# B and C products over 2048 columns, and one tile for the copies of dt·x, in a selective-scan layer

## The chip, the cores and the metric

The kernel runs on one core of a Trainium2 chip. A core has five engines with instruction streams of their own: PE (TensorE, matrix products), DVE (VectorE, elementwise work and scans), ACT (ScalarE, functions such as exp), POOL (GpSimd) and SP (SyncE, which here issues nearly all DMAs). They meet through semaphores. Each engine takes its instructions in a fixed order. The metric is the device time of one execution, in microseconds.

## What is computed

A decoder layer over 8 sequences of 512 tokens with 512 features, in three stages with a residual and a layer norm after each: a selective state-space layer (Mamba), a cross attention with 16 heads, and a mixture of 32 experts. The change lies in the first stage, whose core is this (D_INNER 1024 channels, 16 states a channel):

```python
dt = softplus(dt @ dt_proj_w + dt_proj_b)
dA = exp(A[None, None] * dt[..., None])
dBx = dt[..., None] * B_ssm[:, :, None, :] * x_main[..., None]

def scan_fn(h, inp):
    dA_t, dBx_t, C_t = inp
    h = dA_t * h + dBx_t
    y_t = einsum('bdn,bn->bd', h, C_t)
    return (h, y_t)

y = y + x_main * D_param
y = y * silu(z)
out = res_scale * (y @ out_proj_w) + residual
```

So each of 1024 x 16 states runs through a first-order recurrence over time. Its input is the product of dt·x with B, and its output is multiplied with C and summed over the states.

## The kernel before

**Chunks and steps.** The eight sequences are cut into 16 chunks of T = 256 tokens. A chunk takes 32 steps (q, g, jj): q = 0 to 3 picks 256 channels, g = 0 to 3 picks 4 of the 16 states, jj = 0 or 1 picks half of the channels. A step's tiles have 128 partitions, 32 channels x 4 states, and NB = 4 blocks of 256 tokens, each with one more column ahead of it that carries the old state in. There are 512 steps in all. Two steps that differ in jj alone are called a group here (256 of them), and passing on to the next q a change of q (63 of them).

**A step** consists of these parts:

- `carry` (L484) takes an h tile of 4 x 257 columns (six buffers) and copies the old state into the first column of each block, on ACT.
- `decays` (L475) writes exp(A·dt) into one of two tiles `das`, four ACT instructions over 256 columns (L480).
- `steps_in` (L491) is the B product: dt·x times B into h, on DVE, 1024 columns (L494).
- `scan` (L498) runs the recurrence on DVE over 4 x 257 columns (L501).
- `keep` (L503) saves the last column for the next chunk, on ACT.
- `collect` (L508) is the C product: h times C in place, on DVE, 1024 columns (L510). After the one with jj = 1 it hands back `products` (L516): four matmuls that sum the states of both h tiles with the matrix `fold` into `py` (L521). They are called a step later.

**Copies.** Since a channel lies on four partitions, dt and dt·x are spread by DMA. `prepare` (L432) computes dt and dt·x for 256 channels (its DVE part is L457 to L460) once for each q. `repeat` (L422) then copies them into tiles `rep`, 128 x 1024 columns of 4 bytes, each by two DMAs of 256 KB on SP (L428). For each q there are four such tiles: dt and dt·x, each for jj = 0 and 1. All of them share five buffers. `bcast` (L412) spreads the rows of B and C in a like manner, once a chunk.

**Order.** The main loop (from L1099) writes down in each step: the B product, a third of the side work, the scan, then carry and decays of the next step, another third, the products of the group before, the C product, and the last third. Side work is everything else: projections and convolution of the next chunk, gate and output projection of the chunk before, and the attention of the sequence before (`units`, L753), which has maxima over scores on DVE (L815), exponentials on ACT (L843) and small DMAs on SP (L799 to L803, L829, L875). `repeat` is called at k%8 = 5 and 6, where k counts the steps of a chunk; the next q's first step is k%8 = 0.

This written order is not the order of execution. The tile framework reorders the instructions of each engine when it builds the program: it takes the ready instruction that stands first, by its own estimate of times, and adds all semaphores. So DVE often runs two B products, two scans and two C products in a row.

Of the kernel before, what the change touches and what calls it, by code (L numbers as in the profile page):

```python
# [8 lines left out]
F32 = mybir.dt.float32  # L9
# [3 lines left out]
ALU = mybir.AluOpType  # L13
# [4 lines left out]
P = 128  # L18
# [9 lines left out]
T = 256  # L28
NT_ = T // P
NG = NST // 4  # L30
NQ = 4
QP = P // NQ
NB = 4
# [55 lines left out]
def layers(ctx, tc, a, x1d, filld, based, xbuf):  # L89
# [23 lines left out]
    nc = tc.nc  # L113

    mp = ctx.enter_context(tc.tile_pool(name="l_mamba", bufs=1))
    bcp = ctx.enter_context(tc.tile_pool(name="l_bc", bufs=2 * NST // NG))
    cp = ctx.enter_context(tc.tile_pool(name="l_const", bufs=1))
# [73 lines left out]

    conv_tail = cp.tile([P, CC, 3], F32, name="l_conv_tail")
    state = cp.tile([P, CC // 2, NG, 2, NB], F32, name="l_state")
    nothing = cp.tile([P, NB, 1], F32, name="l_nothing")
    nc.gpsimd.memset(nothing, 0.0)
    das = [mp.tile([P, NB, T + 1], F32, name=f"l_da{i}") for i in range(2)]
    for da in das:
# [30 lines left out]
    first = cp.tile([P, E], F32, name="l_first")  # L228
    nc.gpsimd.iota(first, pattern=[[CAP, E]], base=-SLOTS, channel_multiplier=0, allow_small_or_imprecise_dtypes=True)
    first = first.unsqueeze(1).to_broadcast([P, SC, E])  # L230
# [181 lines left out]
    def bcast(f, g):  # L412

        got = []
        for r0 in (g, NST + g):
            t = bcp.tile([P, T], F32, tag="bc", name="bc")
            src = f["scr"].rearrange("(n s g) t -> n g s t", n=2, s=NQ)[r0 // NST, r0 % NST]
            nc.sync.dma_start(t, src.unsqueeze(0).to_broadcast([QP, NQ, T]))
            got.append(t.unsqueeze(1).to_broadcast([P, NB, T]))
        f["bc", g] = got  # L420

    def repeat(f, q, what, jj):  # L422

        f["rep", what, q, jj] = to = mp.tile([P, 2, 2, T], F32, tag="rep", name="rep", bufs=5)
        for j in range(2):
            r0 = (2 * jj + j) * QP
            src = f["ready", q][what][r0 : r0 + QP].rearrange("c i t -> c (i t)")
            nc.sync.dma_start(  # L428
                to[:, j].rearrange("p i t -> p (i t)"), src.unsqueeze(1).to_broadcast([QP, NQ, 2 * T])
            )  # L430

    def prepare(q, f):  # L432

# [40 lines left out]

    def decays(f, q, g, jj, da):  # L475

        dt = f["rep", 0, q, jj]
        for n in range(NB):
            j, i = n // 2, n % 2
            nc.scalar.activation(  # L480
                da[:, n, 1:], dt[:, j, i, :], AF.Exp, scale=aneg[:, 2 * q + i, 2 * jj + j, g : g + 1]
            )

    def carry(t, q, g, jj):  # L484

        last = state[:, q, g, jj].unsqueeze(2)
        h = mp.tile([P, NB, T + 1], F32, tag="h", name="h", bufs=6)
        nc.scalar.copy(h[:, :, 0:1], last if t else nothing)
        return h

    def steps_in(f, q, g, jj, h):  # L491

        dtx = f.pop(("rep", 1, q, jj)) if g == NG - 1 else f["rep", 1, q, jj]
        nc.vector.tensor_tensor(  # L494
            h[:, :, 1:], dtx.rearrange("p j i t -> p (j i) t"), f["bc", g][0], ALU.mult
        )

    def scan(da, h):  # L498

        flat = h.rearrange("p n t -> p (n t)")  # L500
        nc.vector.tensor_tensor_scan(flat, da.rearrange("p n t -> p (n t)"), flat, 0.0, ALU.mult, ALU.add)  # L501

    def keep(t, q, g, jj, h):  # L503

        if t < S // T - 1:
            nc.scalar.copy(state[:, q, g, jj].unsqueeze(2), h[:, :, T : T + 1])

    def collect(f, q, g, jj, h):  # L508

        nc.vector.tensor_tensor(h[:, :, 0:T], h[:, :, 1:], f["bc", g][1], ALU.mult)  # L510
        if jj == 0:
            f["half"] = h
            return
        hs, xs = (f.pop("half"), h), f["xs"][q]

        def products():  # L516
            if g == 0:
                f["py"] = psy.tile([P, 2, T], F32, tag="py", name="py")
                nc.tensor.matmul(f["py"], ident, xs, start=True, stop=False)
            for j in range(NQ):  # L520
                nc.tensor.matmul(  # L521
                    f["py"][j * QP : (j + 1) * QP, :, :],
                    fold,
                    hs[j // 2][:, 2 * (j % 2) : 2 * (j % 2) + 2, 0:T],
                    start=False,
                    stop=g == NG - 1,
                )

        return products
# [522 lines left out]
    steps = [(q, g, jj) for q in range(CC // 2) for g in range(NG) for jj in range(2)]  # L1052
# [19 lines left out]
    f = {"xt": x0}  # L1072
# [13 lines left out]
    n = 0  # L1086
    for g in range(NG):
        bcast(f, g)
    for what in range(2):
        for jj in range(2):  # L1090
            repeat(f, 0, what, jj)
    nc.scalar.activation(aneg, aneg, AF.Exp)
    nc.vector.tensor_scalar(aneg, aneg, -1.0, None, ALU.mult)
    decays(f, 0, 0, 0, das[0])
    ahead, products = carry(0, 0, 0, 0), None
    old, side, cleared, held = None, [], 0, None
    clock.append(0)

    for i, (b, t) in enumerate(chunks):  # L1099
        nf = {}  # L1100
        after = chunks[i + 1] if i + 1 < len(chunks) else None
# [5 lines left out]
        for k, (q, g, jj) in enumerate(steps):  # L1107
            if i and k == 1:
                bcast(f, NG - 1)
            if after and 28 <= k < 31:  # L1110
                bcast(nf, k - 28)
            qf, nq = (f, q + 1) if q + 1 < CC // 2 else (nf, 0)
            h = ahead

            parts = []

# [35 lines left out]
            def run(m):  # L1152
                clock[0] += 1
                settle()
                for x in thirds[m]:
                    if x[0] is do:
                        do(*x[1:-1], first=x[-1])
                    else:
                        x[0](*x[1:])

            steps_in(f, q, g, jj, h)
            more = qf is f or after
            if k % 8 == 6 and more:
                repeat(qf, nq, 0, 1)
            if k % 8 == 1:
                if k > 1:
                    gated(q - 1, f)
# [8 lines left out]
            if k == 5 and after:  # L1176
                load_x(*after, nf)
            run(0)
            scan(das[n % 2], h)
            n += 1  # L1180

            if k + 1 < len(steps) or after:
                then = steps[(k + 1) % len(steps)]
                ahead = carry(t if k + 1 < len(steps) else after[1], *then)
                decays(f if k + 1 < len(steps) else nf, *then, das[n % 2])
                if k % 8 == 5 and more:
                    repeat(qf, nq, 0, 0)
                    repeat(qf, nq, 1, 0)
                if k % 8 == 6 and more:
                    repeat(qf, nq, 1, 1)  # L1190
            if held:
                keep(*held)
            held = t, q, g, jj, h
            run(1)

            if products:
                products()
            products = collect(f, q, g, jj, h)
            run(2)
            while i < 2 and cleared < E * (i * len(steps) + k - 6) // (2 * len(steps) - 7):  # L1200
                clear(cleared)
# [5 lines left out]
        f = nf  # L1207
# [356 lines left out]
```

## Time and profile before

Three runs took 5404.84, 5407.18 and 5412.16 us, the median is 5407.18. The profiled execution took 5406.28 us; its span from the first to the last instruction is 5404.6 us, with a granted PE clock of 0.935.

| what | us | of the span |
|---|---|---|
| span of the profiled execution | 5404.6 | |
| PE busy | 4672.4 | 86% |
| DVE busy | 4235.9 | 78% |
| ACT busy | 2593.6 | 48% |
| PE weight loads | 2476.6 | 46% |
| POOL busy | 570.3 | 11% |
| DMA, queue of SP | | 41.1% of 16 engines |

The rows of 40 equal slices show where each engine is busy (in tenths; a slice is 135 us):

```profile
PE   6768889788888988988888888789999999999994
DVE  7999899989989989898998998943566555665554
ACT  5566565565656556566565655523222222222223
```

Up to slice 26 the scan section runs, with DVE at 8 or 9 tenths; behind it the experts run with PE at 9 tenths. A group's row in the page gives line, engine, operation, tiles (out<-in), partitions x columns and count, then busy time and the mean duration of one in ns, then the idle time of the engine just before and what ended it. In the timeline, a line with x2 joins two neighbours into one stretch; a bracket gives the idle time ahead of the instruction and who ended it. Matmul records can be missing here and there, so counts of PE are slightly low.

### The profile page before, as it was taken

Reading aid. Unit: us, or ns where it says so; the run is one execution under the profiler, and the core shown is the slowest. Engines: PE = TensorE matmul, PEld = TensorE weight load, DVE = VectorE, ACT = ScalarE, POOL = GpSimd, SP = SyncE. Lnnn points to the kernel's source line nnn. Section 1 sums busy time; section 2 is a strip of 40 time slices with the busy share of each in tenths; the row PEclk is TensorE's granted clock in tenths of the full one; section 3 lists DMA queues with packets and bytes.
Section 4 is the critical chain, followed back from the end, with each engine's and each line's share of the span. In section 5 each row is a group of like instructions: output and inputs, shape, how many; then the busy total and the mean of one; then the engine's idle time right before and its main releaser. Section 6 shows DMA issues by size and latency. Waiting matters only on the chain. (4 is left out here: it accounts for less than half of the span.)

```text
span 5404.6 us, 53991 instructions
## 1 busy us (share of the span) xinstructions
PE 4672.4 (86%) x17320; PEld 2476.6 (46%) x17320; DVE 4235.9 (78%) x5369; ACT 2593.6 (48%) x5726; POOL 570.3 (11%) x426
## 2 busy tenths in 40 slices
PE   6768889788888988988888888789999999999994
PEld 3324234234333423433333342333677777777773
DVE  7999899989989989898998998943566555665554
ACT  5566565565656556566565655523222222222223
POOL 1000002002000200200200020011111111111111
PEclk8879989999999999999999999899999999999997
DMA  8875346345444634634544463342344444544544
GB/s 236 266 224 146 87 96 208 81 114 176 114 104 117 197 77 109 189 98 107 174 125 100 117 200 78 91 146 66 103 128 127 123 117 118 127 127 121 129 115 144
DMA packets 486427, 719.03 MB, mean 133 GB/s; under 512 B 117137, under 2 KB 200625, under 8 KB 484096
## 3 DMA queue, kind: packets, MB, share of 16 engines
q1 hardware_dynamic: 450128, 627.16, 41.1%
q0 software_dynamic: 33280, 76.90, 7.5%
q10 hardware_dynamic: 2736, 11.54, 0.5%
q8 instruction: 137, 2.24, 0.2%
q14 instruction: 146, 1.20, 0.1%
HBM read 391.24 MB, written 165.05 MB: 103 GB/s over the span
## 5 line engine op out<-in xcount | busy, mean ns | idle before, releaser
L480 ACT ACTIVATE l_da<-rep,l_aneg 128x256 f32<-128x256 f32 x2048 | 895.0, 501 | 941.8 <-DVE h L501 877.0
L501 DVE TENSOR_TENSOR_SCAN h<-l_da,h 128x1028 f32<-128x1028 f32 x512 | 1166.0, 2292 | 20.3 <-ACT l_da L480 17.7
L494 DVE TENSOR_TENSOR h<-rep,bc 128x1024 f32<-128x1024 f32 x512 | 614.7, 1218 | 103.1 <-PE py L521 84.6
L510 DVE TENSOR_TENSOR h<-h,bc 128x1024 f32<-128x1024 f32 x512 | 619.5, 1217 | 2.1
L521 PE MATMUL py<-h,l_fold 128*32 128x512 f32 x2048 | 368.3, 644 | 113.4 <-DVE h L510 96.5
L813 PE MATMUL ps_s<-l_ka,l_qa 64*128 64x512 f32 x1024 | 325.6, 707 | 137.8 <-DVE mx L815 137.6
L1314 PE MATMUL ps_h<-xT,w 128*128 128x320 f32 x1536 | 435.8, 433 | 0.0
L1394 POOL DMA_INDIRECT based<-y,xe x160 | 255.5, 1597 | 1309.9 <-ACT y L1417 630.0
L1335 DVE TENSOR_TENSOR hT<-ps_h,p 128x320 f32<-128x320 f32 x128 | 62.9, 492 | 378.5 <-PE ps_h L1314 378.5
L815 DVE TENSOR_REDUCE mx<-ps_s 128x2 f32<-128x1024 f32 x256 | 310.2, 1217 | 58.5 <-PE ps_s L813 58.3
L1314 PEld LDWEIGHTS ps_h<-xT,w 128*128 128x128 f32 x1536 | 292.5, 191 | 118.3 <-issue 0.4
L855 PE MATMUL po<-eT,l_va 128*64 128x512 f32 x1024 | 301.5, 670 | 47.6 <-ACT eT L843 43.1
L839 PE MATMUL ps_t<-l_qa,l_ka 64*128 64x512 f32 x1024 | 308.4, 674 | 23.8 <-ACT eT L843 23.1
L843 ACT ACTIVATE eT<-ps_t 128x1024 f32<-128x1024 f32 x256 | 259.0, 1015 | 128.8 <-PE ps_t L839 128.5
L688 POOL DMA_INDIRECT xbuf<-x2t,dest x128 | 217.2, 1697 | 860.4 <-DVE dest L679 760.8
L1314 PE MATMUL ps_h<-t,s 128*128 128x320 f32 x1024 | 286.1, 432 | 0.0
L343 PE MATMUL ps_z<-xnT,wm 128*128 128x256 f32 x1024 | 238.0, 388 | 30.0 <-DVE o L561 24.3
L750 PE MATMUL ps_p<-x2T,wa 128*128 128x512 f32 x512 | 241.5, 626 | 18.1 <-ACT hT L944 10.4
L552 PE MATMUL po<-wm,zs 128*128 128x512 f32 x512 | 244.7, 632 | 13.8 <-DVE z L957 11.9
L343 PE MATMUL ps_x<-xnT,wm 128*128 128x256 f32 x1024 | 246.5, 393 | 4.5 <-ACT xnT L332 2.5
L343 PEld LDWEIGHTS ps_z<-xnT,wm 128*128 128x128 f32 x1024 | 194.6, 193 | 93.0 <-DVE o L561 37.5
L343 PEld LDWEIGHTS ps_x<-xnT,wm 128*128 128x128 f32 x1024 | 196.1, 195 | 80.5 <-issue 43.8
(232 smaller groups left out, 7170.4 us busy)
## 6 DMA issues: line engine op xcount, KB each, us to landing
w<-in_w SPq DMA_DIRECT2D x93, 1024.0 KB
wm<-in_in_proj_w SPq DMA_DIRECT2D x128, 512.0 KB
rep<-dt SPq DMA_DIRECT2D x256, 256.0 KB
rep<-dtx SPq DMA_DIRECT2D x256, 256.0 KB
xbuf<-zero SPq DMA_DIRECT2D x32, 1362.5 KB
xe<-xbuf SPq DMA_DIRECT2D x32, 1362.5 KB
wm<-in_out_proj_w SPq DMA_DIRECT2D x64, 512.0 KB
wa<-in_sw SPq DMA_DIRECT2D x24, 1024.0 KB
```

Source lines behind the costliest of these rows:

```text
L343: nc.tensor.matmul(ps[:, i, :], w[:, dc, i * P : (i + 1) * P], f["xnT"][:, dc, :], start=(dc == 0), stop=(dc == DC - 1),)
L480: nc.scalar.activation(da[:, n, 1:], dt[:, j, i, :], AF.Exp, scale=aneg[:, 2 * q + i, 2 * jj + j, g : g + 1])
L494: nc.vector.tensor_tensor(h[:, :, 1:], dtx.rearrange("p j i t -> p (j i) t"), f["bc", g][0], ALU.mult)
L501: nc.vector.tensor_tensor_scan(flat, da.rearrange("p n t -> p (n t)"), flat, 0.0, ALU.mult, ALU.add)
L510: nc.vector.tensor_tensor(h[:, :, 0:T], h[:, :, 1:], f["bc", g][1], ALU.mult)
L521: nc.tensor.matmul(f["py"][j * QP : (j + 1) * QP, :, :], fold, hs[j // 2][:, 2 * (j % 2) : 2 * (j % 2) + 2, 0:T], start=False, stop=g == N ...
L813: nc.tensor.matmul(ps[:, j, :], qa[r, lt * P : (lt + 1) * P], ka[r, :], start=True, stop=True)
L815: return lambda: nc.vector.tensor_reduce(mx[:, lt, :].unsqueeze(2), ps, AX.X, ALU.max) and None
L839: nc.tensor.matmul(ps[:, j, :], ka[r, kc * P : (kc + 1) * P], qa[r, :], start=True, stop=True)
L843: nc.scalar.activation(eT, ps, AF.Exp)
L855: nc.tensor.matmul(po[j * 2 * HD : (j + 1) * 2 * HD, :], va[:, kc, i, j * HD : (j + 2) * HD], eT[:, j, :], start=(kc == 0), stop=(kc == SC ...
L1314: nc.tensor.matmul(ps, w[:, n, r * P : (r + 1) * P], x[:, n, :], start=not more and n == 0, stop=n == 1, skip_group_check=more,)
```

## The change

The two steps of a group share one h tile of 2 x 4 blocks (2 x 4 x 257 columns, three buffers). The B product is done once a group, at jj = 0, over 8 x 256 = 2048 columns; the C product once a group, at jj = 1. `carry` and `keep` work on both halves at once, so they too are done once a group. Scans and decays remain single, each on its half of the tile.

The copies of dt keep tiles of 1024 columns (now three buffers). The copies of dt·x for both jj go into one tile `repx` of 2048 columns, with one buffer, by four DMAs that are now written down at k%8 = 6, right behind the B product of g = 3. The copies of dt stay at k%8 = 5 and 6. `products` of the group before are called at jj = 0.

```diff
 
     conv_tail = cp.tile([P, CC, 3], F32, name="l_conv_tail")
     state = cp.tile([P, CC // 2, NG, 2, NB], F32, name="l_state")
-    nothing = cp.tile([P, NB, 1], F32, name="l_nothing")
+    nothing = cp.tile([P, 2, NB, 1], F32, name="l_nothing")
     nc.gpsimd.memset(nothing, 0.0)
     das = [mp.tile([P, NB, T + 1], F32, name=f"l_da{i}") for i in range(2)]
     for da in das:
...
             t = bcp.tile([P, T], F32, tag="bc", name="bc")
             src = f["scr"].rearrange("(n s g) t -> n g s t", n=2, s=NQ)[r0 // NST, r0 % NST]
             nc.sync.dma_start(t, src.unsqueeze(0).to_broadcast([QP, NQ, T]))
-            got.append(t.unsqueeze(1).to_broadcast([P, NB, T]))
+            got.append(t.unsqueeze(1).to_broadcast([P, 2 * NB, T]))
         f["bc", g] = got
 
-    def repeat(f, q, what, jj):
-
-        f["rep", what, q, jj] = to = mp.tile([P, 2, 2, T], F32, tag="rep", name="rep", bufs=5)
-        for j in range(2):
-            r0 = (2 * jj + j) * QP
+    def copies(f, q, what, to, first):
+
+        for j in range(to.shape[1]):
+            r0 = (first + j) * QP
             src = f["ready", q][what][r0 : r0 + QP].rearrange("c i t -> c (i t)")
             nc.sync.dma_start(
                 to[:, j].rearrange("p i t -> p (i t)"), src.unsqueeze(1).to_broadcast([QP, NQ, 2 * T])
             )
+
+    def repeat_dt(f, q, jj):
+
+        f["dt", q, jj] = to = mp.tile([P, 2, 2, T], F32, tag="rep", name="rep", bufs=3)
+        copies(f, q, 0, to, 2 * jj)
+
+    def repeat_dtx(f, q):
+
+        f["dtx", q] = to = mp.tile([P, NQ, 2, T], F32, tag="repx", name="repx")
+        copies(f, q, 1, to, 0)
 
     def prepare(q, f):
 
...
 
     def decays(f, q, g, jj, da):
 
-        dt = f["rep", 0, q, jj]
+        dt = f["dt", q, jj]
         for n in range(NB):
             j, i = n // 2, n % 2
             nc.scalar.activation(
                 da[:, n, 1:], dt[:, j, i, :], AF.Exp, scale=aneg[:, 2 * q + i, 2 * jj + j, g : g + 1]
             )
 
-    def carry(t, q, g, jj):
-
-        last = state[:, q, g, jj].unsqueeze(2)
-        h = mp.tile([P, NB, T + 1], F32, tag="h", name="h", bufs=6)
-        nc.scalar.copy(h[:, :, 0:1], last if t else nothing)
+    def carry(t, q, g):
+
+        h = mp.tile([P, 2, NB, T + 1], F32, tag="h", name="h", bufs=3)
+        nc.scalar.copy(h[:, :, :, 0:1], state[:, q, g].unsqueeze(3) if t else nothing)
         return h
 
-    def steps_in(f, q, g, jj, h):
-
-        dtx = f.pop(("rep", 1, q, jj)) if g == NG - 1 else f["rep", 1, q, jj]
-        nc.vector.tensor_tensor(
-            h[:, :, 1:], dtx.rearrange("p j i t -> p (j i) t"), f["bc", g][0], ALU.mult
-        )
+    def steps_in(f, q, g, h):
+
+        dtx = f.pop(("dtx", q)) if g == NG - 1 else f["dtx", q]
+        wide = h.rearrange("p r n t -> p (r n) t")
+        nc.vector.tensor_tensor(wide[:, :, 1:], dtx.rearrange("p j i t -> p (j i) t"), f["bc", g][0], ALU.mult)
 
     def scan(da, h):
 
         flat = h.rearrange("p n t -> p (n t)")
         nc.vector.tensor_tensor_scan(flat, da.rearrange("p n t -> p (n t)"), flat, 0.0, ALU.mult, ALU.add)
 
-    def keep(t, q, g, jj, h):
+    def keep(t, q, g, h):
 
         if t < S // T - 1:
-            nc.scalar.copy(state[:, q, g, jj].unsqueeze(2), h[:, :, T : T + 1])
-
-    def collect(f, q, g, jj, h):
-
-        nc.vector.tensor_tensor(h[:, :, 0:T], h[:, :, 1:], f["bc", g][1], ALU.mult)
-        if jj == 0:
-            f["half"] = h
-            return
-        hs, xs = (f.pop("half"), h), f["xs"][q]
+            nc.scalar.copy(state[:, q, g].unsqueeze(3), h[:, :, :, T : T + 1])
+
+    def collect(f, q, g, h):
+
+        wide = h.rearrange("p r n t -> p (r n) t")
+        nc.vector.tensor_tensor(wide[:, :, 0:T], wide[:, :, 1:], f["bc", g][1], ALU.mult)
+        xs = f["xs"][q]
 
         def products():
             if g == 0:
...
                 nc.tensor.matmul(
                     f["py"][j * QP : (j + 1) * QP, :, :],
                     fold,
-                    hs[j // 2][:, 2 * (j % 2) : 2 * (j % 2) + 2, 0:T],
+                    wide[:, 2 * j : 2 * j + 2, 0:T],
                     start=False,
                     stop=g == NG - 1,
                 )
...
     n = 0
     for g in range(NG):
         bcast(f, g)
-    for what in range(2):
-        for jj in range(2):
-            repeat(f, 0, what, jj)
+    for jj in range(2):
+        repeat_dt(f, 0, jj)
+    repeat_dtx(f, 0)
     nc.scalar.activation(aneg, aneg, AF.Exp)
     nc.vector.tensor_scalar(aneg, aneg, -1.0, None, ALU.mult)
     decays(f, 0, 0, 0, das[0])
-    ahead, products = carry(0, 0, 0, 0), None
+    ahead, products = carry(0, 0, 0), None
     old, side, cleared, held = None, [], 0, None
     clock.append(0)
 
...
             if after and 28 <= k < 31:
                 bcast(nf, k - 28)
             qf, nq = (f, q + 1) if q + 1 < CC // 2 else (nf, 0)
-            h = ahead
+            if jj == 0:
+                h = ahead
 
             parts = []
 
...
                     else:
                         x[0](*x[1:])
 
-            steps_in(f, q, g, jj, h)
+            if jj == 0:
+                steps_in(f, q, g, h)
             more = qf is f or after
             if k % 8 == 6 and more:
-                repeat(qf, nq, 0, 1)
+                repeat_dtx(qf, nq)
             if k % 8 == 1:
                 if k > 1:
                     gated(q - 1, f)
...
             if k == 5 and after:
                 load_x(*after, nf)
             run(0)
-            scan(das[n % 2], h)
+            scan(das[n % 2], h[:, jj])
             n += 1
 
             if k + 1 < len(steps) or after:
                 then = steps[(k + 1) % len(steps)]
-                ahead = carry(t if k + 1 < len(steps) else after[1], *then)
+                if jj:
+                    ahead = carry(t if k + 1 < len(steps) else after[1], *then[:2])
                 decays(f if k + 1 < len(steps) else nf, *then, das[n % 2])
-                if k % 8 == 5 and more:
-                    repeat(qf, nq, 0, 0)
-                    repeat(qf, nq, 1, 0)
-                if k % 8 == 6 and more:
-                    repeat(qf, nq, 1, 1)
-            if held:
+                if k % 8 in (5, 6) and more:
+                    repeat_dt(qf, nq, k % 8 - 5)
+            if jj == 0 and held:
                 keep(*held)
-            held = t, q, g, jj, h
             run(1)
 
-            if products:
-                products()
-            products = collect(f, q, g, jj, h)
+            if jj == 0:
+                if products:
+                    products()
+            else:
+                held = t, q, g, h
+                products = collect(f, q, g, h)
             run(2)
             while i < 2 and cleared < E * (i * len(steps) + k - 6) // (2 * len(steps) - 7):
                 clear(cleared)
```

## The prediction

> **What bounds the kernel now.** I read the busy table first, then the split of the run into stretches, then the groups of instructions, then the timeline of the scan section. The whole change lies in the scan section, from the first scan at 63 us to the last at 3522 us.
>
> ```profile
> 63.00:3522.00 3459.00, 2859.45 (x10158) 1218.26 (x10156) 3185.29 (x3382) 2043.15 (x4598) 271.93 (x191) 0.92 0.51 138
> ```
>
> This row of the stretch view holds, after the length, busy time of PE, weight loads, DVE, ACT and POOL, then the granted PE clock 0.92 and the DMA share. DVE works 3185 of 3459 us (92%), PE 83%, ACT 59%. The remaining 1883 us (experts, last norm) contain nothing that is edited. So DVE is the bound here; its three big rows are the ones touched:
>
> ```profile
> L501 DVE TENSOR_TENSOR_SCAN h<-l_da,h 128x1028 f32<-128x1028 f32 x512 | 1166.0, 2292 | 20.3 <-ACT l_da L480 17.7
> L494 DVE TENSOR_TENSOR h<-rep,bc 128x1024 f32<-128x1024 f32 x512 | 614.7, 1218 | 103.1 <-PE py L521 84.6
> L510 DVE TENSOR_TENSOR h<-h,bc 128x1024 f32<-128x1024 f32 x512 | 619.5, 1217 | 2.1
> ```
>
> Mean durations are 2292, 1218 and 1217 ns. DVE waits hardly at all before scans and C products; before B products it waits 103 us, mostly until PE has read an old h tile.
>
> **Merging the products: -38 us.** 512 B products and 512 C products become 256 and 256, so 512 merges. No 2048-column product is in the trace. The row of the product dt·x (L460, 512 columns) says 685 ns, L494 says 1218 for 1024, so 533 ns per 512 columns and 1218 + 2 x 533 = 2284 ns for 2048. Two products alone would be 2435 ns, a saving of 151. But neighbours on DVE overlap, as the timeline shows where two or more are joined in one line:
>
> ```profile
> 1381.27 2.35 DVE L494 TENSOR_TENSOR h<-rep,bc 128x1024 f32<-128x1024 f32 x2
> 1383.54 4.49 DVE L501 TENSOR_TENSOR_SCAN h<-l_da,h 128x1028 f32<-128x1028 f32 x2
> 1387.94 0.73 DVE L735 SCALAR_TENSOR_TENSOR k<-ps_p,l_bk,mk 128x512 f32<-128x512 f32 x1
> 1388.58 2.35 DVE L510 TENSOR_TENSOR h<-h,bc 128x1024 f32<-128x1024 f32 x2
> 1390.85 1.22 DVE L494 TENSOR_TENSOR h<-rep,bc 128x1024 f32<-128x1024 f32 x1
> 1393.32 1.23 DVE L494 TENSOR_TENSOR h<-rep,bc 128x1024 f32<-128x1024 f32 x1 [1.25 <-DMA rep<-dtx]
> ```
>
> Two products take 2.35 us, not 2.44. A merge saves 2.35 - 2.28 = 0.07 to 0.08 us; 512 x 0.075 = 38 us. Bounds: 35 (only the 92% of the time in which DVE works) and 77 (512 x 0.151). I take 38, because neighbours are the rule in this section.
>
> [...]
>
> **Order within a group: +14 us.** Program order is product, scan, product; the trace shows DVE in another order, B B scan scan C C or mixtures, so that neighbours mostly do not depend on each other. Where they do, it costs:
>
> ```profile
> 1496.62 1.22 DVE L510 TENSOR_TENSOR h<-h,bc 128x1024 f32<-128x1024 f32 x1
> 1497.75 2.30 DVE L501 TENSOR_TENSOR_SCAN h<-l_da,h 128x1028 f32<-128x1028 f32 x1
> 1500.08 1.22 DVE L510 TENSOR_TENSOR h<-h,bc 128x1024 f32<-128x1024 f32 x1
> ```
>
> The scan starts 0.09 us before the unrelated product ends; the product that needs this scan starts 0.03 us after its end: 0.12 us more. Where a scan directly follows its own B product it starts 0.10 us after it: 0.19 us more. Going through the section's DVE timeline I count 60 and 16 such pairs of 512 each, some 10 us. With one B product, two scans and one C product per group there are 256 possible pairs of each kind, and fewer other instructions to put between. Lowest: none is left, -10 us. Highest: all, 256 x (0.12 + 0.19) = 79, +69 us. I take the pair at each of the 63 changes of q, where the next B product can't be pulled forward (below): 63 x 0.31 = 20; and today's 7.4% of the other 386 pairs at 0.155: 4. 24 - 10 = +14.
>
> [...]
>
> **The copies of dt·x: +24 us.** Today the five rep buffers let the copies for the next q start while the old tile is in use. One repx tile (8 KB a partition) has no spare: its four copies of 256 KB wait until the B product of g = 3 has finished, and the B product of the next q waits for all four. What DVE has to do in between is the cover. I added it up on the timeline for each of the 63 changes of q: everything between the B products at k%8 = 6 and the next q's first, plus scans and C products of that group that today come after it. In the first ten changes it is 7.3 to 10.5 us; later it repeats every eight: 12.8, 7.3, 14.1, 11.9, 10.3, 10.1, 14.0 and 10.0 us. Against that, the copies. At the start, with nothing else on SyncE, four are issued from 54.59 us and the second B product has them at 61.8 us: 7.2. In the section:
>
> ```profile
> 1382.52 2.42 SPq L428 DMA_DIRECT2D rep<-dt  x2
> 1385.03 3.64 SPq L428 DMA_DIRECT2D rep<-dtx  x2
> ```
>
> The last of these four ended the 1.25 us wait at 1393.32: 10.8 us. If the need is 8 us, the shortfalls add up to 6 us; at 9 to 17; at 10 to 30; at 11 to 62; at 12 to 99. I take 10, nearer to the loaded row; today's waits for rep<-dtx in the section (6.5 us) go away: 30 - 6.5 = +24. Bounds -6 and +93. Behind the waiting B product stand both scans; ACT's decays wait for those (877 us already), and PE's products for the C product. On SyncE, in order, the copies of dt for jj = 1, the weights and the maxima wait behind the four copies; the last gate PE's scores.
>
> **Coarser steps: +15 us.** A B or C product now holds DVE 2.28 us, so whatever waits behind it waits up to 1.1 us longer. 35 times B waits for PE's products (84.6 us), whose first half could have begun after one C product: 0 to 39 us. PE waits 95 times for the maxima (137 us); half of those behind a wide product, half of 1.1 us each: 0 to 27. Upper end 66; most falls into time when PE has other work: 15.
>
> **Costed at about nothing.** ACT loses 256 carries and 128 keeps of about 0.19 us, 73 us; it is hidden, since ACT sits waiting for scans. If ACT were the cover, at most the 18 us that scans wait for decays would be won. dt's three buffers still hold two live tiles and a spare. PE issues the same matmuls. Start: the first B product needs the last copy: +1 us, once.
>
> **The sum.** -38 + 14 + 24 + 15 + 1 = +16. The profiled run took 5406.3 (span 5404.6 and 1.7 around it), the median is 5407.2, so they agree within 1 us: 5406.3 + 16 = 5422.
>
> **Rivals.** First, it is faster: the next B product is put between scan and C product whenever a spare h tile exists, so dependent pairs stay at today's number, and the copies meet a need of 9 us: -38 + (17 - 6.5) + 1 = -27, 5379. For it: today's order already separates 93% of the pairs, and an early B product also starts the copies earlier. Against: three double h tiles instead of six single ones, and 84.6 us of waits for them already. It decides when the four copies land within 9 us.
>
> Second, nothing is gained or lost: DVE has 274 us of waits for PE and ACT in the section, and the 38 us turn into longer waits there, as the stalls fall into existing ones. About 5405. Against: 92% busy leaves few such places.
>
> Third, much slower: SyncE is late. At 1493 to 1501 us its queue issues without a break, and two dt·x copies go out 8 us after the B product. With a need of 12 us everywhere: +99 - 6.5 - 38 + 14 + 15 + 1 = +85, 5491.
>
> **Chances.** Forecast 0.38, faster 0.33, no change 0.17, much slower 0.12. A difference under 0.2% (11 us) can't be told from none here. So faster by more 0.33, within 0.17, slower by more 0.38 + 0.12 = 0.50. The range goes from just under the faster case, 5372, to the much slower one, 5490; the forecast's own range is 5400 to 5455.
>
> **What would show it.** The products' rows should be x256 at 2284 ns. DVE busy in the section should fall by 35 to 45 us. If the third term is right, the wait of the B product for the copies of dt·x appears with 20 to 40 us in the list of waits, at changes of q; under 10 us speaks for the first rival, over 80 for the third. Scans that start 0.1 us after their own B product show the second term. The prediction is wrong if DVE's idle time in the section does not grow: then only the 38 us are left, and it is faster.

## The result and the profile after

The changed kernel takes 5491.57 us (median of four runs, 5490.11 to 5493.52), the kernel before 5406.01 (four runs). The ratio is 1.0158, its 95% interval 1.0141 to 1.0176: 85.6 us slower. The forecast was 16 us slower, and the result lies 1.6 us above the top of the range.

The groups of the page after, in the same columns as before:

```profile
L508 DVE TENSOR_TENSOR_SCAN h<-l_da,h 128x1028 f32<-128x1028 f32 x512 | 1158.9, 2286 | 10.2 <-ACT l_da L489 4.3
L503 DVE TENSOR_TENSOR h<-repx,bc 128x2048 f32<-128x2048 f32 x256 | 583.3, 2282 | 181.0 <-PE py L526 124.0
L518 DVE TENSOR_TENSOR h<-h,bc 128x2048 f32<-128x2048 f32 x256 | 585.3, 2286 | 3.5
```

There are 256 products of each kind at 2282 and 2286 ns, as worked out (2284). The idle time ahead of the B products went from 103.1 to 181.0 us. The stretch from the first scan to the last, in the view by windows (length, then busy time of PE, weight loads, DVE, ACT and POOL):

```profile
66.02:3592.93 3526.91, 2858.26 (x10109) 1222.85 (x10107) 3161.77 (x2859) 2006.86 (x4207) 319.25 (x191) 0.91 0.48 135
```

DVE works 24 us less than before (3161.8 against 3185.3) and the stretch is 68 us longer, so DVE stands idle 365 us instead of 274. PE's work is unchanged (2858.3 against 2859.5). Another 3 us are lost ahead of the first scan and 14 behind the last. The list of waits of DVE over the whole run, each with its sum, how often, and the longest:

```profile
DVE h L503 <- PE py L526: 124.0, 39, 7.1
DVE mx L820 <- PE ps_s L818: 82.9, 45, 3.0
...
DVE zs L540 <- PE py L526: 48.4, 26, 3.5
...
DVE h L503 <- DMA repx<-dtx: 33.6, 12, 5.9
```

Inside the section, B waits for PE 124 us instead of 85, the gate (`zs`) 48 instead of 2, the maxima 39 instead of 14, and B for the copies of dt·x 34 instead of 6.5. These sums show where DVE stands; which part of the change puts it there they don't show.

### The profile page after: what moved, and what is told of

The parts are those of the page before. It is cut to its first block, busy times and chain, and to the rows that moved or that the text cites. A ratio compares the mean times of both kernels' runs of the same rounds, so it can differ in the third digit from the quotient of the medians.

```text
span 5489.9 us, 52851 instructions
## 1 busy us (share of the span) xinstructions
PE 4688.8 (85%) x17320; PEld 2488.2 (45%) x17320; DVE 4217.5 (77%) x4857; ACT 2563.2 (47%) x5341; POOL 618.6 (11%) x426
## 5 line engine op out<-in xcount | busy, mean ns | idle before, releaser
L508 DVE TENSOR_TENSOR_SCAN h<-l_da,h 128x1028 f32<-128x1028 f32 x512 | 1158.9, 2286 | 10.2 <-ACT l_da L489 4.3
L503 DVE TENSOR_TENSOR h<-repx,bc 128x2048 f32<-128x2048 f32 x256 | 583.3, 2282 | 181.0 <-PE py L526 124.0
L518 DVE TENSOR_TENSOR h<-h,bc 128x2048 f32<-128x2048 f32 x256 | 585.3, 2286 | 3.5
L526 PE MATMUL py<-h,l_fold 128*32 128x512 f32 x2048 | 356.9, 668 | 154.1 <-DVE h L518 112.2
L693 POOL DMA_INDIRECT xbuf<-x2t,dest x128 | 239.2, 1869 | 894.7 <-DVE dest L684 469.5
L343 PE MATMUL ps_z<-xnT,wm 128*128 128x256 f32 x1024 | 249.0, 402 | 34.0 <-DVE o L566 23.0
```

What stands on the lines that cost most here:

```text
L343: nc.tensor.matmul(ps[:, i, :], w[:, dc, i * P : (i + 1) * P], f["xnT"][:, dc, :], start=(dc == 0), stop=(dc == DC - 1),)
L503: nc.vector.tensor_tensor(wide[:, :, 1:], dtx.rearrange("p j i t -> p (j i) t"), f["bc", g][0], ALU.mult)
L518: nc.vector.tensor_tensor(wide[:, :, 0:T], wide[:, :, 1:], f["bc", g][1], ALU.mult)
L526: nc.tensor.matmul(f["py"][j * QP : (j + 1) * QP, :, :], fold, wide[:, 2 * j : 2 * j + 2, 0:T], start=False, stop=g == NG - 1,)
```

## The experiments

Each kernel was timed in turn with the kernel before on one chip. The kernel before had a median of 5402.7 to 5405.0 us in the five sets.

### Tiles, B and C one at a time (e1 to e4)

Three theories stood at the outset. A: the single tile of dt·x costs, since its copies can't start early. B: the wide C product hands h to PE late, and the wide B product gets it back late. C: the framework's order of instructions came out worse by chance. e1 keeps the shared h tile, the common carry and keep, and nothing else: B and C are single again, at their old places, with the five `rep` buffers. The diffs of this part are against the changed kernel:

```diff
-        nc.vector.tensor_tensor(wide[:, :, 1:], dtx.rearrange("p j i t -> p (j i) t"), f["bc", g][0], ALU.mult)
+        nc.vector.tensor_tensor(
+            h[:, jj, :, 1:], dtx.rearrange("p j i t -> p (j i) t"), f["bc", g][0][:, 0:NB, :], ALU.mult
+        )
...
-        nc.vector.tensor_tensor(wide[:, :, 0:T], wide[:, :, 1:], f["bc", g][1], ALU.mult)
+        nc.vector.tensor_tensor(h[:, jj, :, 0:T], h[:, jj, :, 1:], f["bc", g][1][:, 0:NB, :], ALU.mult)
+        if jj == 0:
+            return
```

> h in tiles of eight blocks, carry and keep once a group, but both products still over 1024 columns and dt x in the five rep buffers. Theory A (the loss comes from the single dt x tile, which keeps the next q's B product from starting early): 5406 plus or minus 15, little idle before zs. Theory B (the loss comes from h in three pairs, whose release by PE comes later): 5435 to 5470, and the wait of the B product for PE's products stays at 110 us or more. Theory C (any new order costs about that much): 5440 to 5500.

Measured: 5405.3 us, ratio 0.9999 (0.9986 to 1.0011). The pair of tiles, three of them instead of six, costs nothing.

e2 takes the second hunk only (B wide from the one tile, C single):

> As e1, and the B product over 2048 columns from the single dt x tile; the C product still over 1024. Theory A: 5470 to 5500, with 25 to 45 us of waits for the copies of dt x and 30 us or more before zs. Theory B, in the form that the wide C product hands its tile to PE late: within 20 us of e1.

Measured: 5445.3, ratio 1.0072 (1.0046 to 1.0097), 40 above e1, with 31.5 us of waits for the copies. This lies between what A and B had given.

e3 takes the first hunk only (C wide, B single from five buffers):

> As e1, and the C product over 2048 columns; B over 1024 columns from the five rep buffers. Theory A: 5385 to 5410, since 256 merges save 10 to 20 us and nothing waits. Theory B: 5450 to 5490, with the waits of B for PE's products and of zs for py as long as with the whole change (124 and 48 us).

Measured: 5498.2, ratio 1.0175 (1.0158 to 1.0192), more than the whole change and above the ranges of A and B. B waits 151 us for PE, and 35 us for copies of dt·x that are made late in DVE's new order.

e4 is the whole change without the copies:

```diff
-        f["dtx", q] = to = mp.tile([P, NQ, 2, T], F32, tag="repx", name="repx")
-        copies(f, q, 1, to, 0)
+        if "x" not in first_dtx:
+            first_dtx["x"] = to = mp.tile([P, NQ, 2, T], F32, tag="repx", name="repx")
+            copies(f, q, 1, to, 0)
+        f["dtx", q] = first_dtx["x"]
```

> The whole change, but dt x is copied for the first q alone; every later q uses that tile, so the copies and the waits for them are left out. Theory A: 5380 to 5415, the idle time before zs under 15 us. Theory B: 5450 or more, since h and the products are as in the whole change.

Measured: 5455.6, ratio 1.0097 (1.0080 to 1.0114), 36 below the changed kernel. At this point theory A seemed to explain 36 to 40 us and the wide C product the rest. What was missing was the same edit in the kernel before.

### Yardsticks for the copies and for the hand-over (e5 to e8)

e5 is e2 with e4's edit. e6 is the kernel before, with two tiles for dt·x that are filled once:

```diff
+        if what and (what, jj) in first_dtx:
+            f["rep", what, q, jj] = first_dtx[what, jj]
+            return
...
```

> As e2 (wide B product from one dt·x tile, single C products), but dt·x is copied for the first q alone, so later B products use its values again; DVE, ACT and PE have the same instructions as in e2 (5445). If the single tile's copies are all of e2's cost: 5445 - 40 = 5405, or less by the 19 us that 256 merged B products save (5386). If the wide B product costs by itself, by the order or by the coarser step: over 5425. The B products' wait for the copies (31.5 us) is gone in either case.

> The kernel before with dt·x copied for the first q alone, in tiles of its own; later B products use its values again. It is the yardstick for e4 and e5: what the copies cost in the kernel before. By its trace 6.5 us of waits, so 5398. If copies cost in general (queue, memory), well under 5390. If the whole change costs nothing but its copies, e4 (5455.6) would be 38 below this one; if the wide C product costs by itself, e4 is some 50 above it.

Measured: e5 5412.8, ratio 1.0020 (1.0010 to 1.0030); e6 5374.9, ratio 0.9945 (0.9929 to 0.9962). The copies cost 28 us in the kernel before too, though its trace shows only 6.5 us of waits for them. It is hardly a matter of the order: of the 3380 instructions that DVE works off between the first scan and the last, 3338 come in the same order in e6. So the copies alone explain 36 - 28 = 8 us of the change, a difference of four medians and little more than their scatter, and without any copies the change still costs 5455.6 - 5374.9 = 81. Theory A falls: e5 stands 38 above e6 with no copies in either.

e7 and e8 cut the tie between DVE and PE: the matmuls read a tile of ones.

```diff
-                    wide[:, 2 * j : 2 * j + 2, 0:T],
+                    ones.unsqueeze(1).to_broadcast([P, 4, P]),
```

> The kernel before, but the matmuls of the products over states read a tile of ones in place of h: as many matmuls over as many columns, only nothing passes from the C products to PE, nor from PE back to the B products; the output leaves out the states' part. It is the yardstick for e8. The waits of B for PE's products (84.6 us) go; as part of them come back at other places: 5340 to 5400.

> The same in the changed kernel: the products over states read ones, not h. If the wide C product costs by handing h to PE late and getting it back late, this hand-over is gone: it stands 20 to 45 us above e7 (the copies of dt·x alone, perhaps less the merging). If the order or the wide instructions themselves cost, it stands 80 or more above e7, as the changed kernel above the one before. If merging saves 38 us and the hand-over was all: equal to e7 or below.

Measured: e7 5553.9, ratio 1.0278 (1.0261 to 1.0296); e8 5609.0, ratio 1.0377 (1.0360 to 1.0394). No expectation foresaw that the yardstick would become 151 us slower. The first wait of B in e7's list:

```profile
DVE h L494 <- DMA rep<-dtx: 201.6, 56, 10.2
```

Without the tie the framework puts DVE's work in another order (1550 of the 3380 instructions between the first scan and the last come in the same order as before), and dt·x comes late in it. That the order is the cause is likely, but not shown. The difference of 55 us between the two can't be read as the hand-over, since both wait for something new. The pair is inconclusive.

### More h tiles, and products earlier (e9 to e12)

In e9 and e10 the B product takes the row of C in place of dt·x, which frees the room for a fourth pair (`bufs=4`), or for eight single tiles in the kernel before:

```diff
-        h = mp.tile([P, 2, NB, T + 1], F32, tag="h", name="h", bufs=3)
+        h = mp.tile([P, 2, NB, T + 1], F32, tag="h", name="h", bufs=4)
```

> The changed kernel with a fourth pair of h tiles. To make room, dt·x is not copied and has no tile: the B product multiplies the row of C with the row of B, same size, type and engine. It is read against e4 (three pairs, no copies, 5455.6) and e10. If the cost is that the wide B product must wait until PE has read a whole old pair and there are three of them: 40 to 80 less than e4, 5375 to 5415; the waits of B for PE's products (138.7 us) fall under 60. If the wide instructions or the order cost by themselves: over 5435.

> The kernel before with eight single h tiles instead of six, and the same B product without dt·x: the yardstick for e9, and against e6 (six tiles, no copies, 5374.9). If h tiles are short before as well, 5310 to 5360, with the waits of B for PE (97.8 us) under 40; if those waits only move to other places, 5360 to 5376. With enough tiles the merged products should count at last: e9 below e10 by 24 (the busy time that DVE saved) to 38. If e9 is above e10 by 40 or more, the number of tiles is not the cause.

Measured: e9 5507.8, ratio 1.0192 (1.0175 to 1.0209); e10 5407.4, ratio 1.0010 (0.9999 to 1.0021). Both became slower than with fewer tiles (e4 5455.6, e6 5374.9), e10 beyond all that was expected of it. Since the B product's operand was exchanged as well, the difference can't be put down to the tiles alone. The waits of e9:

```profile
DVE h L501 <- PE py L524: 135.4, 45, 7.1
...
DVE h L506 <- ACT l_da L488: 64.4, 27, 7.5
```

B waits for PE as long as with three pairs (138.7 in e4), and scans now wait for decays as well. So the number of tiles doesn't set the wait, and the first half of theory B falls.

e11 and e12 call the products of the group before at the start of the next group (shown for the changed kernel):

```diff
+            if jj == 0 and products:
+                products()
             run(0)
...
-            if jj == 0:
-                if products:
-                    products()
-            else:
+            if jj:
```

> The changed kernel with the products of the group before called at the start of the next group, ahead of the side work of its first step, so that PE hands the h pair back sooner. If B waits for PE because the products stand behind side matmuls in PE's order: 20 to 60 less than the changed kernel, 5430 to 5470, and the waits of B for PE fall under 80 us (124.0). If PE then stands waiting for the wide C product instead: 5490 or more, with PE's own waits for h (134.5 and 112.2 us) longer.

> The same edit in the kernel before (5405). If it is a gain of the hand-over alone, it is smaller here than in e11: 0 to 25 less. If it gains as much as in e11, lateness of the products has nothing to do with the wide products, only with the order.

Measured: e11 5504.8, ratio 1.0195 (1.0177 to 1.0212); e12 5475.1, ratio 1.0130 (1.0113 to 1.0146). In e11 the waits of B for PE did fall, to 73 us, but those for the copies rose to 80 within the section. For e12 a gain had been expected. Not one of its instructions differs from the kernel before, only the written place of four matmuls a group (eight records in the trace), and it is 70 us slower; 2468 of DVE's 3380 instructions come in the same order. A change of order can thus cost nearly as much as the whole change; theory C was now the likeliest.

### Width or place (e13 to e16)

The change does two things at once to a product: it doubles its width, and it moves half of it. The B product of the second half stands a step earlier in the written order, the C product of the first half a step later. e13 undoes the width alone, at the changed places, with all else of the change kept:

```diff
-        nc.vector.tensor_tensor(wide[:, :, 1:], dtx.rearrange("p j i t -> p (j i) t"), f["bc", g][0], ALU.mult)
+        for r in range(2):
+            nc.vector.tensor_tensor(h[:, r, :, 1:], dtx[:, 2 * r : 2 * r + 2].rearrange("p j i t -> p (j i) t"), f["bc", g][0][:, 0:NB, :], ALU.mult)
...
-        nc.vector.tensor_tensor(wide[:, :, 0:T], wide[:, :, 1:], f["bc", g][1], ALU.mult)
+        for r in range(2):
+            nc.vector.tensor_tensor(h[:, r, :, 0:T], h[:, r, :, 1:], f["bc", g][1][:, 0:NB, :], ALU.mult)
```

> The changed kernel, with each product over 2048 columns written as two over 1024 at the same place (second B product at jj = 0, first C product at jj = 1). Copies, tiles and all else stay. If the width costs (others wait for an instruction of 2.28 us, h comes late): back to 5405 to 5430. If the changed places and the order that follows from them cost: 5490 or more, up to 5530 by the 38 us that merging saved. DVE's busy time rises by some 25 us in both cases.

e14 does the first of these two in e5:

> e5 (wide B product, single C, no copies: 5412.8) with the B product written as two at the same place, jj = 0. Against e6, which has them a step apart (5374.9). Width: back to 5370 to 5385. Place: 5413 to 5432.

e15 and e16 disturb the written order of the side work in both kernels:

```diff
-        return (clock[0] + 3 if clock else 0), part
+        return (clock[0] + 4 if clock else 0), part
```

> The kernel before, with the follow-up of a side unit written four thirds of a step behind it instead of three; same instructions, another order. If the time follows from the order, it moves by 20 us or more, likely up, as e12 did (+70). If the order matters little: 5395 to 5415.

> The same in the changed kernel (5491.6). If the cost is a chance of the order, the difference to e15 is not 86 but anything from 0 to 150. If the wide products cost by their width in any order: e15 + 70 to 100.

Measured: e13 5406.2, ratio 1.0003 (0.9994 to 1.0013). Splitting the products wins back the whole cost: places, the pair, the one tile of dt·x and its later copies together cost nothing as long as the products are short. What the framework makes of the width is part of this. Apart from the products DVE has 2358 instructions between the first scan and the last of e13, and 2080 of them come in the same order in the changed kernel; the rest it put elsewhere. e14 5384.0, ratio 0.9958 (0.9944 to 0.9972): without copies, the width of B is 5412.8 - 5384.0 = 29 of its 38 us, the place 9. e15 5410.3 (1.0014, 1.0004 to 1.0024) and e16 5497.0 (1.0168, 1.0147 to 1.0188): in this other order (2563 of the changed kernel's 2858 instructions of DVE in the section come in the same order) the changed kernel is still 87 us behind. So the cost does not hang on the one order that the changed kernel happened to get; two orders are few, and e12 shows that an order alone can cost 70 us.

The rows and the window of e13, to be held against those of the changed kernel:

```profile
L504 DVE TENSOR_TENSOR h<-repx,bc 128x1024 f32<-128x1024 f32 x512 | 612.0, 1221 | 141.4 <-PE py L528 125.1
...
L520 DVE TENSOR_TENSOR h<-h,bc 128x1024 f32<-128x1024 f32 x512 | 611.8, 1216 | 0.3
```

```profile
62.74:3513.95 3451.21, 2868.84 (x10141) 1216.90 (x10139) 3176.75 (x3379) 2005.56 (x4212) 299.95 (x191) 0.91 0.50 138
```

From e13 to the changed kernel the spans differ by 84.7 us (5405.2 and 5489.9): DVE's busy time falls by 15.0, its idle time in the section rises by 90.7, the start adds 3.3 and the end 5.7. In e13 B waits 125 us for PE, just as long as in the changed kernel (124). The largest wait of the list was thus not the one that grew with the width. What grew is B's wait for the copies (4.7 to 33.6), the gate's for PE (31.6 to 48.4), the maxima's (25.7 to 38.6) and that of `dtx` for ACT (36.1 to 48.0).

Where the loss lies can be read from the scans. The first 64, one sequence, take 336.9 us in the changed kernel and 338.3 in e13 (333.3 in the kernel before): there the wide products cost nothing against narrow ones. No maximum of the attention runs yet (the first one starts at 527 us), and B waits only once, 1.1 us, for a copy of dt·x. The next 64 take 449.0 and 446.5 us, and each sequence from the third on is 9.6 to 16.7 us longer than in e13.

Two places show how. First the attention scores. The same stretch of DVE's timeline, from the same pair of scans to the next B product, in the changed kernel:

```profile
1539.21 4.48 DVE L508 TENSOR_TENSOR_SCAN h<-l_da,h 128x1028 f32<-128x1028 f32 x2
1543.72 2.29 DVE L518 TENSOR_TENSOR h<-h,bc 128x2048 f32<-128x2048 f32 x1
1545.93 1.22 DVE L820 TENSOR_REDUCE mx<-ps_s 128x2 f32<-128x1024 f32 x1
1549.02 1.23 DVE L820 TENSOR_REDUCE mx<-ps_s 128x2 f32<-128x1024 f32 x1 [1.87 <-PE ps_s L818]
1553.33 2.29 DVE L503 TENSOR_TENSOR h<-repx,bc 128x2048 f32<-128x2048 f32 x1 [3.09 <-PE py L526]
```

and in e13:

```profile
1514.38 4.48 DVE L509 TENSOR_TENSOR_SCAN h<-l_da,h 128x1028 f32<-128x1028 f32 x2
1518.77 1.20 DVE L520 TENSOR_TENSOR h<-h,bc 128x1024 f32<-128x1024 f32 x1
1519.89 1.22 DVE L822 TENSOR_REDUCE mx<-ps_s 128x2 f32<-128x1024 f32 x1
1521.02 1.22 DVE L520 TENSOR_TENSOR h<-h,bc 128x1024 f32<-128x1024 f32 x1
1522.77 1.23 DVE L822 TENSOR_REDUCE mx<-ps_s 128x2 f32<-128x1024 f32 x1 [0.53 <-PE ps_s L820]
1527.26 2.36 DVE L504 TENSOR_TENSOR h<-repx,bc 128x1024 f32<-128x1024 f32 x2 [3.27 <-PE py L528]
```

In e13 the first maximum slips between the two C products and starts 5.51 us after the start of the scans; behind the wide product it starts at 6.72. PE's timeline shows what follows, in the changed kernel:

```profile
1547.21 0.27 PE L827 MATMUL ps_m<-l_ident,mx 128*2 128x128 f32 x1 [3.46 <-DVE mx L820]
1547.45 1.54 PE L818 MATMUL ps_s<-l_ka,l_qa 64*128 64x512 f32 x4
...
1552.22 1.06 PE L526 MATMUL py<-h,l_fold 128*32 128x512 f32 x6
```

and in e13:

```profile
1521.16 0.27 PE L829 MATMUL ps_m<-l_ident,mx 128*2 128x128 f32 x1 [3.23 <-DVE mx L822]
1521.37 1.36 PE L820 MATMUL ps_s<-l_ka,l_qa 64*128 64x512 f32 x4
...
1526.13 1.06 PE L528 MATMUL py<-h,l_fold 128*32 128x512 f32 x8
```

PE transposes the maximum (`ps_m`) and computes the next scores (`ps_s`); the second maximum on DVE waits for these (1.87 instead of 0.53). The products for the old h stand behind them in PE's order, and B waits for the products: it starts 14.12 us after the scans instead of 12.88. The 1.2 us come out at the end undiminished, although the wait in the bracket is even shorter than in e13. Two rounds on stands one of the largest waits of the section:

```profile
1592.59 2.29 DVE L503 TENSOR_TENSOR h<-repx,bc 128x2048 f32<-128x2048 f32 x1 [7.03 <-PE py L526]
```

Such a wait of 7.0 to 7.1 us comes once in each sequence but the first; in e13 it is 5.6 at the same seven places. PE's timeline ahead of it, in the changed kernel:

```profile
1581.68 1.24 PE L818 MATMUL ps_s<-l_ka,l_qa 64*128 64x512 f32 x4 [3.72 <-DVE mx L820]
1582.85 7.81 PE L557 MATMUL po<-wm,zs 128*128 128x512 f32 x14
1590.50 1.02 PE L524 MATMUL py<-xs,l_ident 128*128 128x512 f32 x2
1591.45 1.06 PE L526 MATMUL py<-h,l_fold 128*32 128x512 f32 x8
```

PE sits 3.72 us until a maximum on DVE is done (2.67 at this place in e13), then works off 7.8 us of the output projection, and only then the products that B waits for. A late maximum moves all of this. The sixteen steps around it (q = 3 and q = 0 of the next chunk) take 133.6 us in this kernel and 125.5 in e13, from first scan to first scan (1477.78 to 1611.37, and 1455.41 to 1580.87). This is a stretch with much of the loss; other stretches lose less, and some gain.

Second, the copies of dt·x. SP's and DVE's timelines of the changed kernel at a change of q:

```profile
1347.38 0.54 SPq L427 DMA_DIRECT2D repx<-dtx  x1
1348.02 2.60 SPq L159 DMA_DIRECT2D wm<-in_in_proj_w  x1
1350.67 2.69 SPq L427 DMA_DIRECT2D repx<-dtx  x2
1353.46 2.19 SPq L159 DMA_DIRECT2D wm<-in_in_proj_w  x1
1355.69 1.50 SPq L427 DMA_DIRECT2D repx<-dtx  x1
```

```profile
1364.39 2.29 DVE L503 TENSOR_TENSOR h<-repx,bc 128x2048 f32<-128x2048 f32 x1 [5.87 <-DMA repx<-dtx]
```

The old B product ends at 1347.35, the first copy goes out at once, but weights stand between the four in SP's queue, and the last one is issued at 1355.69. The wide B product needs all four: 17.0 us from one B product to the next. In e13 the weights stand there too, but the first half needs two copies:

```profile
1343.93 1.23 DVE L504 TENSOR_TENSOR h<-repx,bc 128x1024 f32<-128x1024 f32 x1 [2.34 <-PE py L528]
1345.37 1.23 DVE L504 TENSOR_TENSOR h<-repx,bc 128x1024 f32<-128x1024 f32 x1 [0.21 <-DMA repx<-dtx]
```

It waits for PE until 1343.93, not for a copy, and the second half is held up by 0.21 us. It starts 14.8 us after the old B product, against 17.0. Part of that is SP's queue, whose order differs: from the first to the last of the four copies it takes 6.7 us there and 8.3 here.

### Each product alone (e17, e18)

e17 splits B alone in the changed kernel, e18 C alone; the diffs are the two halves of e13's.

> The changed kernel with the B product alone written as two at its place; C stays wide. Between e13 (both split, 5406.2) and the changed kernel (5491.6). Without copies the wide B was worth 29 (e5 - e14); with copies it must also wait for all four of them, 37 us of waits, most of which a split B avoids: 50 to 65 less, 5427 to 5442. If only the width of C counts: 5480 or more.

> The changed kernel with the C product alone written as two at its place; B stays wide. Without copies the wide C was worth 43 (e4 - e5): 5440 to 5455. If the costs of B and C add up, the gains of e17 and e18 make 85 together; if one wide product is enough for the delay, they make much less (each under 25); if removing one removes most of the delay, much more.

Measured, at the changed places, with the one tile of dt·x:

| | B as two of 1024 | B of 2048 |
|---|---|---|
| C as two of 1024 | 5406.2 (e13) | 5433.1 (e18), ratio 1.0053 (1.0036 to 1.0069) |
| C of 2048 | 5419.2 (e17), ratio 1.0032 (1.0021 to 1.0043) | 5491.6 (the change) |

Both came out lower than expected. Wide C alone costs 13 us, wide B alone 27, both together 85. They don't add up: 45 us appear only when both are wide. Splitting either one wins back most, 72 or 59 us. In e18 B's waits for the copies are 36 us, in e17 they are 2, which fits that the single tile costs only a wide B product. That both lie on one loop (scans, C, PE, B) and that each alone still finds some slack there would explain the 45 us; this is argued, not shown.

Left open is e3: it too has a wide C and single B products, yet is 79 us slower than e17. It differs in the place of the second B product and in the five buffers. The order may play a part there, as in e12; this stays open. No version beat the kernel before: e1 and e13 equal it, and those that are faster leave out the copies.

## Why the prediction was off

**Merging, -38 us.** The durations were right to 2 ns. DVE's busy time fell by 24 us against the kernel before, and by 15 against e13, whose products stand at the same places. The form (some hundredths of a microsecond for each merge, because neighbours overlap; two B products in a row take 2.36 us in e13, not 2.44) was right, its size somewhat too large. The 15 us are a net figure: the changed kernel has 101 C products directly behind their own scan and 49 scans directly behind their own B product, e13 has 8 and none, and each such pair gives up the 0.09 us by which neighbours overlap, some 13 us by this estimate. Without that the merges would save about 28. The prediction's bound of 77 us, a saving for each merge of the whole 151 ns by which two durations exceed a wide one's, is refuted more clearly still.

**Order within a group, +14.** C products directly behind their own scan went from 60 to 101 and scans directly behind their own B product from 16 to 49. By the prediction's own prices that is 41 x 0.12 + 33 x 0.19 = 11 us. Right in kind and size, as a count priced by the trace.

**The copies, +24.** The expected waits were 30 us, the trace has 33.6. As time they come to far less, about 8 us (e4 and e6), since the kernel before pays for its copies as well. They are not spread over the changes as assumed: 12 waits, about two in each sequence from the third on, one of about 1 and one of 3.5 to 5.9 us. The cause of the larger, weights between the copies in SP's queue, is the mechanism of the third rival, at one change in eight and not everywhere. And the blame was put on the tile that has no spare; e13 keeps this tile and has 4.7 us of waits. It is the wide product's need for all four copies.

**Coarser steps, +15: the step that failed.** It named the right thing, work that waits behind an instruction of 2.28 us, and the maxima for which PE waits. It then halved the delay of each, and took 15 of 66 on the ground that most falls into time when PE has other work. Between e13 and the changed kernel idle time in the section grows by 90.7 us. Of these 28.9 are waits for the copies, and about 8 lie at dependent neighbours (93 x 0.03 + 49 x 0.10); some 54 are left for this term, more than three times its 15 and close to its upper end. That it is not the copies is shown more directly by e4 and e6: with none in either kernel the change still costs 81 us. The delay isn't shed at the next engine: in the attention scores, DVE and PE pass work back and forth, and 1.2 us lost at a maximum are still 1.2 us when the next B product starts. Nor does a sum over the waits of the old trace bound this well, since the waits move: B's wait for PE grew by 40 us in e13 without any loss of time.

**Start +1, end 0.** Measured 3 and 14. The sum has no term for the end. Of the 14 us behind the last scan 9 are there in e13 as well. PE is busy there for 1785.9 us, against 1769.7 before and 1775.9 in e13, so more of its work is left over for the end; which work stays open.

**The rivals.** The third gave 5491, the time that was measured, but by stalls for the copies at every change (99 us, found 33.6). Its number was right and its reason only at one place. The first rival (copies within 9 us, dependent pairs as before) is excluded: at the place above B needs 17.0 us, the waits are 33.6 us where it has 17, and the dependent pairs grew from 60 and 16 to 101 and 49. The second (DVE's savings end in longer waits, no change) has the right picture of the savings, and e13 shows such a shift of waits at equal time, but it priced the new waits at no more than the savings. The stated sign of a wrong forecast, no growth of DVE's idle time, did not appear; idle time grew by 91 us and busy time fell by 24.

## What to carry to other kernels

Where two engines hand work back and forth, as DVE and PE do here, the length of an instruction can be a delay for everything that could have gone in its middle: behind the wide product a maximum started 6.72 us after the scans instead of 5.51, and the next B product 14.12 instead of 12.88. Ask of each merge which short instruction used to slip between the two halves, who waits for it, and whether the loop returns to the merging engine; if it does, count the full delay for each round, not half of it (with half delays, taken in part, this term was put at 15 us, and some 54 were left for it). A wide consumer also turns a transfer in parts into one that must be complete (B waits 33.6 us for its copies, and 4.7 in e13). To tell width from place, split the wide instruction again where it stands. And test the suspected cost in the old kernel too; the copies cost 28 us there, which made them look like the culprit.

## What had not been expected

- Two fp32 products over 1024 columns instead of one over 2048 cost DVE only 15 us of busy time for 512 pairs (0.03 us a pair, net of the overlap that the changed kernel loses at dependent neighbours), although twice 1221 ns is 160 ns more than 2282.
- The copies of dt·x cost the kernel before 28 us with 6.5 us of waits for them. In e6 the waits for other transfers, such as 6.3 us for `xr` and 2.7 for `xt`, vanish with them.
- With more buffers, and another operand for B, both kernels were slower (e9 against e4 52 us, e10 against e6 32), and taking a dependence away made the kernel before 151 us slower (e7), in another order of the framework's.
